# Layer 3 attention: score groups of three heads across key tiles, one exponential over three PSUM banks

## Chip, cores and metric

The kernel runs on one core of one Trainium2 chip. The metric is the device time of one execution in microseconds; it is the time from the first to the last instruction of that core, plus a few microseconds of start.

## The reference

Four layers, each added to its input `x` of shape (2, 128, 64, 64). Only the last one is touched. It normalizes `x` by groups, projects it to queries, keys and values of eight heads with 16 channels each, and attends over all S = 4096 places:

```python
def _L3_conv_ref(x, wq, bq, wk, bk, wv, bv):
    ...
    a = jnp.einsum('bhcq,bhck->bhqk', q, k) / jnp.sqrt(jnp.float32(C))
    a = jax.nn.softmax(a, axis=-1)
    o = jnp.einsum('bhqk,bhck->bhcq', a, v)
    return o.reshape(B, C, h, w)
...
x = x + _L3_conv_ref(_gn(x), L3_conv_wq, L3_conv_bq, L3_conv_wk, L3_conv_bk, L3_conv_wv, L3_conv_bv)
```

## The kernel before

Layer 3 starts at about 2290 us of the span and lasts to its end. `_layer3` goes through four attentions one after the other: batch b in 0, 1 and half t in 0, 1, a half being four of the eight heads. For each, `queries_and_keys` makes `q` (two tiles, the rounded query and its remainder) and `k`, in which head j lies in the partitions 32j to 32j + 31; `values` makes `vt`, the transposed values, each head with a block of ones beside it, so that the sum of the weights comes out of the same matmul.

`attend` then loops over 8 blocks of 512 queries (qb) and, inside, over 32 tiles of 128 keys (kt): 256 key tiles per attention, 1024 in all. A key tile has three steps.

- `scores` (matmul at L2060): for both query parts n and the four heads j, keys (32 partitions by 128 columns, stationary) times queries (32 by 512, moving). n = 0 starts a sum and n = 1 ends it. Two PSUM tiles `ps_s` of two banks each take the four heads' results. The four matmuls of one n use four different strips of 32 rows of the array.
- the exponential (L2070, ScalarE): one activation for each of the two PSUM tiles, 128 partitions by 1024 columns, to a tile `weights` in SBUF.
- `multiply` (L2079): for the four heads, values (128 partitions by 32 columns, stationary) times weights (128 by 512), added up over the 32 key tiles in one bank of `ps_acc`; head j uses columns 32j to 32j + 31 of the array.

PSUM has three score tiles of two banks (pool `f3_sp`) and two accumulators of one bank (`f3_acc`). Eight `weights` tiles of two banks' size stand in SBUF (`f3_p`).

The order of the instructions on each engine is that of the program: `_in_order` chains them. So TensorE gets, per key tile, the scores of kt and then the value matmuls of kt − 2:

```python
waiting.append((qb, kt, scores(qb, kt)))
if len(waiting) > 2:
    multiply(*waiting.pop(0))
yield kt if over else None
```

The preparation of the next attention is put between: before each even kt one step of `early` (the first attention's remaining keys and values), and at kt 4, 12 and 20 one step of `work()`, which yields the values (L2014), the queries and keys (L1988) and `bound`. At the end of a block of queries, `done` copies the accumulator out (L2101), divides by the sums (L2103 to L2105), adds the residual (L2106) and stores 4 pieces with DMAs of SyncE (L2108). At the end of an attention the value matmuls that still wait are issued, and the next one begins.

Of the kernel before, what the change touches and what calls it, by code (L numbers as in the profile page):

```python
# [10 lines left out]
F32 = mybir.dt.float32  # L11
AF = mybir.ActivationFunctionType
ALU = mybir.AluOpType
AX = mybir.AxisListType
PSUM = bass.MemoryType.PSUM
# [3 lines left out]
CH = 512  # L19
NCH = S // CH  # L20
ROWS = CH // W
NQT = S // 128
# [1894 lines left out]
    nc.vector.tensor_scalar_mul(l3["b_qk"], l3["b_qk"], scales)  # L1917


@with_exitstack  # L1920
def _layer3(ctx, tc, X, l3, cst, out, worst, here):
    nc = tc.nc
# [2 lines left out]
    ctx.enter_context(_in_order(tc))  # L1925
    one = ctx.enter_context(tc.tile_pool(name="f3_one", bufs=1))
    two = ctx.enter_context(tc.tile_pool(name="f3_two", bufs=2))
    pp = ctx.enter_context(tc.tile_pool(name="f3_p", bufs=8))
    spp = ctx.enter_context(tc.tile_pool(name="f3_sp", bufs=3, space=PSUM))
    accp = ctx.enter_context(tc.tile_pool(name="f3_acc", bufs=2, space=PSUM))  # L1930

    def acc():
        return accp.tile([128, CH], F32, tag="acc", name="ps_acc")
# [118 lines left out]
    def attend(b, t, q, k, vt, early):  # L2052
        ac = [None]

        def scores(qb, kt):
            ps = [spp.tile([128, 2, CH], F32, tag="sp", name="ps_s") for _ in range(2)]
            for n in range(2):
                for j in range(4):
                    rows = slice(32 * j, 32 * j + 32)
                    nc.tensor.matmul(  # L2060
                        ps[j // 2][:, j % 2, :],
                        k[rows, kt * 128 : (kt + 1) * 128],
                        q[n][rows, qb * CH : (qb + 1) * CH],
                        start=(n == 0),
                        stop=(n == 1),
                    )
            w = []
            for p in range(2):
                w.append(pp.tile([128, 2, CH], F32, tag="weights", name="weights"))
                nc.scalar.activation(w[p], ps[p], AF.Exp)  # L2070
            return w

        def multiply(qb, kt, w):
            if kt == 0:
                ac[0] = acc()
            for j in range(4):

                i = j % 2
                nc.tensor.matmul(  # L2079
                    ac[0][32 * j : 32 * j + 32, :],  # L2080
                    vt[:, kt, j // 2, i : i + 2, :].rearrange("p a d -> p (a d)"),
                    w[j // 2][:, i, :],
                    start=(kt == 0),
                    stop=(kt == NQT - 1),
                )
            if kt == NQT - 1:
                done(qb, ac[0])

        def done(qb, ps):
            cols = slice(qb * CH, (qb + 1) * CH)  # L2090

            places = [
                (slice(32 * j + 16 * (j % 2), 32 * j + 16 * (j % 2) + 16),
                 slice(64 * t + 16 * j, 64 * t + 16 * j + 16))
                for j in range(4)
            ]
            xs = residual[qb % 2]
            for to, rows in places:
                nc.sync.dma_start(xs[to, :], X[rows, b, cols])
            u = two.tile([128, CH], F32, tag="u", name="u", bufs=1)  # L2100
            nc.vector.tensor_copy(u, ps)  # L2101
            r = two.tile([128, CH], F32, tag="r", name="r", bufs=1)
            nc.vector.stream_shuffle(r, u, [(i + 16) % 32 for i in range(32)])  # L2103
            nc.vector.reciprocal(r, r)  # L2104
            nc.vector.tensor_mul(u, u, r)  # L2105
            nc.vector.tensor_add(u, u, xs)  # L2106
            for at, rows in places:
                nc.sync.dma_start(out[b, rows, cols], u[at, :])  # L2108

        waiting = []  # L2110
        for qb in range(NCH):
            for kt in range(NQT):
                if kt % 2 == 0:
                    over = next(early, early) is early
                waiting.append((qb, kt, scores(qb, kt)))
                if len(waiting) > 2:
                    multiply(*waiting.pop(0))
                yield kt if over else None
        for x in waiting:
            multiply(*x)  # L2120

    def in_turn(*gens):
        gens = list(gens)
# [44 lines left out]
    while found:  # L2168
        b, t, got = found.pop()
        beside = up_to_next(side)  # L2170
        for kt in attend(b, t, *got):

            if kt in (4, 12, 20):
                next(beside, None)
        for _ in beside:
            pass
# [34 lines left out]
def kernel(ctx, tc, a, out):  # L2211
# [4 lines left out]
    with tc.tile_pool(name="keep", bufs=1) as keep:  # L2216
        X, cst, eps5 = _inputs(tc, keep, a)

        worst = keep.tile([128, 1 + 2 * B], F32, name="worst")
        st = keep.tile([128, B + 2, 2], F32, name="st")  # L2220
        rows_of_weights = _layer0(tc, X, a, cst, worst, st[:, :B], dram)
        with tc.tile_pool(name="late", bufs=1) as late:
            with tc.tile_pool(name="raw", bufs=1) as raw:
                l3 = _layer3_inputs(nc, late, raw, a, a["consts2"])
                _layer1(tc, X, a, cst, st[:, :B], st[:, B])
                _layer2(
                    tc,
                    X,
                    rows_of_weights,
                    cst,  # L2230
                    a["consts1"],
                    st[:, B],
                    st[:, B + 1],
                    lambda: _layer3_weights(nc, l3),
                )
            _layer3(tc, X, l3, cst, out, worst, st[:, B + 1])
        with tc.tile_pool(name="flag_ps", bufs=1, space=PSUM) as fp:
            most = keep.tile([128, 1], F32, name="most")
            nc.vector.tensor_reduce(most, worst, AX.X, ALU.max)
            pt = fp.tile([1, 128], F32, name="ps_most")  # L2240
            nc.tensor.transpose(pt, most, cst["ident"])
            top = keep.tile([1, 1], F32, name="top")
            nc.vector.tensor_reduce(top, pt, AX.X, ALU.max)
            nc.vector.tensor_scalar(within, top, LIMIT, None, ALU.is_le)
# [61 lines left out]
```

## Time and profile before

| | |
|---|---|
| time, median of 3 runs | 4274.81 us (4273.35 to 4276.23) |
| profiled execution | 4264.27 us, span 4262.5 us |
| TensorE busy | 4050.0 us, 95% of the span |
| ScalarE busy | 3340.0 us, 78% |
| VectorE busy | 2185.9 us, 51% |
| mean granted TensorE clock | 0.981 |

PE is TensorE's matmuls, PEld its weight loads, which overlap the matmuls; ACT is ScalarE, DVE is VectorE. A line of a group gives the source line, engine and operation, output and inputs with shapes, the count, then the busy time and the mean duration of one instruction, and after the second bar the idle time of the engine just before them, with what ended it. In the timeline a row gives start, length of the merged stretch, engine, line, operation and count; the length reaches to the modelled end of the last matmul, which overlaps the start of the next, so distances between starts are the better measure. A value matmul leaves two records, a score matmul one.

### The profile page before, as it was taken

To read this page: it belongs to the slowest core of one execution; us is meant where nothing else is said; L and a number is where in the kernel's file an instruction comes from. 1 tells how busy PE (TensorE), PEld (TensorE's weight loads), DVE (VectorE), ACT (ScalarE), POOL (GpSimd) and SP (SyncE) were. 2 spreads that over 40 slices of the span, in tenths; PEclk is the share of its full clock that TensorE was granted. 3 is DMA by queue.
4 is the path that set the end of the run, shared out by engine and by line. 5 is a ranking of instruction groups with operands and counts; after the bars stand their busy time and mean duration, and the time that the engine had idled before them with its cause. 6 is when DMAs were issued, how large, how long until landed. Compare 5 with 4: busy or idle time off the path is not lost. (4 is left out here: it accounts for less than half of the span.)

```text
span 4262.5 us, 82256 instructions
## 1 busy us (share of the span) xinstructions
PE 4050.0 (95%) x35790; PEld 1547.6 (36%) x35790; DVE 2185.9 (51%) x2358; ACT 3340.0 (78%) x4051; POOL 68.3 (2%) x145
## 2 busy tenths in 40 slices
PE   6899999979999997997898999999999999999998
PEld 3522222245222223444565333333333333333332
DVE  3679999836899998995775211321132012211111
ACT  4378888734888884334655999999999999999998
POOL 1001000000000001000000000000000000000000
PEclk9999999989999999998999999999999999999999
DMA  1099960000000000002670000000000000000000
GB/s 48 2 183 187 186 98 1 1 1 2 1 1 1 1 1 12 1 1 100 273 286 4 6 4 6 6 6 4 6 6 6 4 6 6 6 4 6 6 6 4
DMA packets 158822, 158.86 MB, mean 37 GB/s; under 512 B 24809, under 2 KB 148713, under 8 KB 154354
## 3 DMA queue, kind: packets, MB, share of 16 engines
q1 hardware_dynamic: 158450, 153.50, 15.2%
q8 instruction: 282, 4.62, 0.4%
q14 instruction: 90, 0.74, 0.1%
HBM read 145.09 MB, written 73.40 MB: 51 GB/s over the span
## 5 line engine op out<-in xcount | busy, mean ns | idle before, releaser
L2070 ACT ACTIVATE weights<-ps_s 128x1024 f32<-128x1024 f32 x2048 | 1884.8, 1097 | 62.8 <-PE ps_s L2060 62.3
L1330 ACT ACTIVATE weights<-ps_s 128x1024 f32<-128x1024 f32 x1024 | 992.5, 1022 | 173.2 <-PE ps_s L1321 148.2
L2079 PE MATMUL ps_acc<-weights,vt 128*32 128x512 f32 x8192 | 1092.8, 605 | 0.0
L2060 PE MATMUL ps_s<-q,k 32*128 32x512 f32 x8192 | 924.8, 444 | 5.4 <-ACT weights L2070 5.4
L1769 DVE TENSOR_TENSOR sums<-sums,weights 128x2048 f32<-128x2048 f32 x384 | 879.0, 2289 | 42.2 <-ACT weights L1330 6.2
L2060 PEld LDWEIGHTS ps_s<-q,k 32*128 32x128 f32 x8192 | 471.1, 182 | 839.4 <-ACT weights L2070 773.6
L1321 PE MATMUL ps_s<-q,k 32*128 32x512 f32 x4096 | 644.9, 640 | 3.6 <-ACT weights L1330 2.2
L2101 DVE COPY u<-ps_acc 128x512 f32<-128x512 f32 x32 | 22.1, 691 | 1039.0 <-PE ps_acc L2079 1039.0
L1734 PE MATMUL ps_acc<-weights,vt 128*32 128x512 f32 x4096 | 548.9, 605 | 3.4 <-ACT used L1759 3.2
L1321 PEld LDWEIGHTS ps_s<-q,k 32*128 32x128 f32 x4096 | 209.4, 183 | 429.7 <-issue 212.5
L2079 PEld LDWEIGHTS ps_acc<-weights,vt 128*32 128x32 f32 x8192 | 162.9, 108 | 379.4 <-issue 367.3
L1734 PEld LDWEIGHTS ps_acc<-weights,vt 128*32 128x32 f32 x4096 | 81.0, 108 | 395.1 <-issue 377.0
L655 DVE SCALAR_TENSOR_TENSOR X<-g,w,X 128x2048 f32<-128x2048 f32 x84 | 197.3, 2350 | 2.4
L1769 DVE TENSOR_TENSOR sums<-weights 128x2048 f32<-128x2048 f32 x64 | 146.5, 2289 | 60.5 <-ACT weights L1330 60.5
L1525 PE MATMUL ps_sp<-pad,diag 32*32 32x512 f32 x4608 | 166.9, 607 | 3.8 <-DVE q L1536 2.3
L988 PE MATMUL ps_z<-w_ri,e 128*32 128x128 f32 x2048 | 137.4, 408 | 13.9 <-DVE e L930 11.8
L2021 DVE TENSOR_TENSOR vt<-ps_acc,bv 128x384 f32<-128x384 f32 x32 | 17.8, 556 | 246.0 <-PE ps_acc L2014 246.0
L1503 PE MATMUL ps_sp<-xn,w_qkv 128*128 128x512 f32 x160 | 92.9, 719 | 33.7 <-DVE k L1536 16.2
L1525 PEld LDWEIGHTS ps_sp<-pad,diag 32*32 32x32 f32 x4608 | 96.1, 104 | 62.4 <-issue 16.9
L1991 DVE LOAD_MASK_SELECT qq<-ps_acc x32 | 0.4, 14 | 222.4 <-PE ps_acc L1988 222.4
L2104 DVE RECIPROCAL r<-r 128x512 f32<-128x512 f32 x32 | 107.3, 3353 | 1.1
L930 DVE TENSOR_SCALAR e<-ps_pe 32x136 f32<-32x136 f32 (+1 forms) x352 | 104.4, 297 | 5.0
(286 smaller groups left out, 2590.5 us busy)
## 6 DMA issues: line engine op xcount, KB each, us to landing
w_ri<-w_r SPq DMA_DIRECT2D x16, 2112.0 KB, 8.1
w_ri<-w_i SPq DMA_DIRECT2D x16, 2112.0 KB, 13.5
w_r<-in_L_conv_kr_w SPq DMA_DIRECT2D x15, 528.0 KB, 12.7
w_r<-in_L_conv_kr_x SPq DMA_DIRECT2D x15, 528.0 KB, 12.5
w_r<-in_L_conv_kr_y SPq DMA_DIRECT2D x15, 528.0 KB, 12.2
w_r<-in_L_conv_kr_z SPq DMA_DIRECT2D x15, 528.0 KB, 12.5
w_i<-in_L_conv_ki_w SPq DMA_DIRECT2D x15, 528.0 KB, 13.1
w_i<-in_L_conv_ki_x SPq DMA_DIRECT2D x15, 528.0 KB, 12.3
```

The lines of the kernel that those rows point to most:

```text
L655: nc.vector.scalar_tensor_tensor(xi, g[:, i : i + H // 2, j : j + W], w8[:, s : s + 1], xi, ALU.mult, ALU.add)
L930: nc.vector.tensor_scalar_mul(out, got[of, :, s], sign)
L988: nc.tensor.matmul(out.rearrange("p (n f o) -> p n f o", n=2, f=2), e[:, s, 2 * j : 2 * j + 2, :].rearrange("p f x -> p (f x)"), w.rearran ...
L1321: nc.tensor.matmul(ps[j // 2][:, j % 2, :], k[rows, kt * 128 : (kt + 1) * 128], q[rows, qb * CH : (qb + 1) * CH], start=True, stop=True,)
L1330: nc.scalar.activation(w[:, 2 * p : 2 * p + 2, :], ps[p], AF.Exp)
L1525: nc.tensor.matmul(ps[r // 2][to, r % 2, :].rearrange("p (h w) -> p h w", w=W), diag[rows, grp, t, :], pad[rows, y0 : y0 + ROWS, t % 3 : t ...
L1734: nc.tensor.matmul(ac[n][rows, :], lhs(rows), w[:, j, :], start=first, stop=last)
L1769: nc.vector.tensor_add(parts[0].rearrange("p j c -> p (j c)"), t.rearrange("p j c -> p (j c)"), w.rearrange("p j c -> p (j c)"),)
L2060: nc.tensor.matmul(ps[j // 2][:, j % 2, :], k[rows, kt * 128 : (kt + 1) * 128], q[n][rows, qb * CH : (qb + 1) * CH], start=(n == 0), stop= ...
L2070: nc.scalar.activation(w[p], ps[p], AF.Exp)
L2079: nc.tensor.matmul(ac[0][32 * j : 32 * j + 32, :], vt[:, kt, j // 2, i : i + 2, :].rearrange("p a d -> p (a d)"), w[j // 2][:, i, :], star ...
L2104: nc.vector.reciprocal(r, r)
```

## The change

The heads of successive key tiles become one stream, (qb, kt, j) with j fastest, cut into groups of three. A group may hold heads of two key tiles. `scores` makes one group: its six matmuls (two query parts, three heads) write one PSUM tile of three banks, and one activation over 1536 columns makes its weights. There are 341 such groups and one of a single head (512 columns) in each attention. `multiply` still takes the four heads of a key tile together, when all four belong to groups older than the previous one. The score pool has two tiles of three banks in place of three of two; the weights pool has five tiles of three banks' size in place of eight of two. The steps of the preparation are tied to the group in which a key tile's head 0 lies.

```diff
-    pp = ctx.enter_context(tc.tile_pool(name="f3_p", bufs=8))
-    spp = ctx.enter_context(tc.tile_pool(name="f3_sp", bufs=3, space=PSUM))
+    pp = ctx.enter_context(tc.tile_pool(name="f3_p", bufs=5))
+    spp = ctx.enter_context(tc.tile_pool(name="f3_sp", bufs=2, space=PSUM))
...
-        def scores(qb, kt):
-            ps = [spp.tile([128, 2, CH], F32, tag="sp", name="ps_s") for _ in range(2)]
-            for n in range(2):
-                for j in range(4):
+        def scores(group):
+
+            n = len(group)
+            ps = spp.tile([128, 3, CH], F32, tag="sp", name="ps_s")
+            for half in range(2):
+                for i, (qb, kt, j) in enumerate(group):
                     rows = slice(32 * j, 32 * j + 32)
                     nc.tensor.matmul(
-                        ps[j // 2][:, j % 2, :],
+                        ps[:, i, :],
                         k[rows, kt * 128 : (kt + 1) * 128],
-                        q[n][rows, qb * CH : (qb + 1) * CH],
-                        start=(n == 0),
-                        stop=(n == 1),
+                        q[half][rows, qb * CH : (qb + 1) * CH],
+                        start=(half == 0),
+                        stop=(half == 1),
                     )
-            w = []
-            for p in range(2):
-                w.append(pp.tile([128, 2, CH], F32, tag="weights", name="weights"))
-                nc.scalar.activation(w[p], ps[p], AF.Exp)
-            return w
+            w = pp.tile([128, 3, CH], F32, tag="weights", name="weights")
+            nc.scalar.activation(w[:, :n], ps[:, :n], AF.Exp)
+            return [w[:, i, :] for i in range(n)]
...
-                    w[j // 2][:, i, :],
+                    w[j],
...
-        waiting = []
-        for qb in range(NCH):
-            for kt in range(NQT):
+        heads = [(qb, kt, j) for qb in range(NCH) for kt in range(NQT) for j in range(HEADS3)]
+        waiting, over = [], False
+
+        def number(qb, kt, j):
+            return (qb * NQT + kt) * HEADS3 + j
+
+        for at in range(0, len(heads) + 2 * GROUP3, GROUP3):
+            group = heads[at : at + GROUP3]
+            begun = [kt for _, kt, j in group if j == 0]
+            for kt in begun:
                 if kt % 2 == 0:
                     over = next(early, early) is early
-                waiting.append((qb, kt, scores(qb, kt)))
-                if len(waiting) > 2:
-                    multiply(*waiting.pop(0))
+            if group:
+                waiting += zip(group, scores(group))
+            while len(waiting) >= HEADS3 and number(*waiting[HEADS3 - 1][0]) < at - GROUP3:
+                four, waiting = waiting[:HEADS3], waiting[HEADS3:]
+                multiply(*four[0][0][:2], [w for _, w in four])
+            for kt in begun:
                 yield kt if over else None
-        for x in waiting:
-            multiply(*x)
```

More of the change, by code (lines that the diff above doesn't have):

```diff
@@ L1917, in _layer3_weights @@
     nc.vector.tensor_scalar_mul(l3["b_qk"], l3["b_qk"], scales)
+HEADS3 = 4
+GROUP3 = 3
 @with_exitstack
```

## Prediction

> **What bounds the kernel now.** I read the page's groups first, then the stretch table over layer 3, then the timeline inside it. Layer 3's attention is 2048 exponentials (L2070), 8192 score matmuls (L2060) and the value matmuls (L2079, two records to a matmul):
>
> ```profile
> L2070 ACT ACTIVATE weights<-ps_s 128x1024 f32<-128x1024 f32 x2048 | 1884.8, 1097 | 62.8 <-PE ps_s L2060 62.3
> L2079 PE MATMUL ps_acc<-weights,vt 128*32 128x512 f32 x8192 | 1092.8, 605 | 0.0
> L2060 PE MATMUL ps_s<-q,k 32*128 32x512 f32 x8192 | 924.8, 444 | 5.4 <-ACT weights L2070 5.4
> ```
>
> ScalarE idles 62.8 us in all; but PE has no idle time either. One row per pair of batch and head half (b, t) says the same (columns: length, then busy us of PE, PEld, DVE, ACT, POOL, granted clock):
>
> ```profile
> 2796.00:3285.00 489.00, 485.31 (x4178) 169.30 (x4180) 103.63 (x158) 470.66 (x512) 0.55 (x1) 1.00 0.02 6
> 3285.00:3773.00 488.00, 486.46 (x4168) 168.61 (x4162) 96.21 (x135) 469.94 (x511) 0.00 (x0) 0.99 0.02 6
> ```
>
> Both engines are over 95% busy, so busy shares cannot say which one sets the pace. The timeline can. Steady state, then an interruption at 3417.08 by one `values` block (L2014):
>
> ```profile
> 3413.59 0.73 PE L2060 MATMUL ps_s<-q,k 32*128 32x512 f32 x6
> 3414.25 1.07 PE L2079 MATMUL ps_acc<-weights,vt 128*32 128x512 f32 x8
> 3415.25 0.47 PEld L2060 LDWEIGHTS ps_s<-q,k 32*128 32x128 f32 x8 [0.84 <-ACT weights L2070]
> 3415.25 0.91 PE L2060 MATMUL ps_s<-q,k 32*128 32x512 f32 x8
> 3416.09 1.06 PE L2079 MATMUL ps_acc<-weights,vt 128*32 128x512 f32 x8
> 3417.08 1.13 PE L2014 MATMUL ps_acc<-wv,X 128*128 128x96 f32 x8
> 3418.14 0.74 PE L2060 MATMUL ps_s<-q,k 32*128 32x512 f32 x8
> 3418.81 1.07 PE L2079 MATMUL ps_acc<-weights,vt 128*32 128x512 f32 x8
> 3418.98 3.77 ACT L2070 ACTIVATE weights<-ps_s 128x1024 f32<-128x1024 f32 x4 [0.86 <-PE ps_s L2060]
> 3419.81 0.98 PE L2060 MATMUL ps_s<-q,k 32*128 32x512 f32 x8
> 3420.72 1.06 PE L2079 MATMUL ps_acc<-weights,vt 128*32 128x512 f32 x8
> 3421.71 0.91 PE L2060 MATMUL ps_s<-q,k 32*128 32x512 f32 x8
> ```
>
> Read the starts. In steady state a key tile costs 1.83 us: scores to values 0.84, values to next scores 1.00; over 14 tiles (2397.06 to 2422.73 in the same view) it is 1.8336. The scores' weight loads wait there for exponentials, two per tile, so one exponential costs 0.917 and **ScalarE sets the pace**. After the interruption every exponential is ready, and PE runs free: scores to values 0.67 (3418.14 to 3418.81), values to scores 1.00 (to 3419.81), 1.67 in all. So PE is only 0.16 us per tile behind ScalarE. A gain on ScalarE beyond 9% would meet PE; a loss on PE beyond 0.16 us per tile makes PE the bound.
>
> Between two (b, t) scores follow scores, which before does only there:
>
> ```profile
> 2796.07 0.96 PE L2060 MATMUL ps_s<-q,k 32*128 32x512 f32 x10
> 2796.90 3.77 ACT L2070 ACTIVATE weights<-ps_s 128x1024 f32<-128x1024 f32 x4 [1.87 <-PE ps_s L2060]
> 2797.97 0.73 PE L2060 MATMUL ps_s<-q,k 32*128 32x512 f32 x6 [0.95 <-ACT weights L2070]
> ```
>
> From scores to their exponential 0.83; that first exponential takes 1.02 by itself, and the scores waiting for its banks start 0.05 after its end (2796.90 + 1.02 + 0.05 = 2797.97). In a narrower window the first eight matmuls last 0.74, the first four 0.51; ten last 0.96. So a round of four heads takes 0.23 (0.74 − 0.51), and the next tile follows within 0.22 when its bank is free.
>
> **What the Trainium skill says.** "TensorEngine Tiling (Array Packing)", Key Properties: tiles in different places work independently and in parallel, and a change of tiling mode drains the engine. "TensorE: Matmul & The Clock Gate", Measured speedup vs the span model: a pack lasts as long as one matmul plus about 4 ns for each further tile. The trace agrees: two of these matmuls that start together last 0.50 (3419.81), four 0.51. So a pack of three costs what a pack of four costs. "ScalarE: Activation LUTs", What ACT_TABLE_LOAD costs: an activation takes 186 ns + 0.833 ns per element, and successive ones overlap by 93 ns. The trace gives 1.02 for 1024 elements (the page 1.04) and 0.917 back to back (0.946 by the page); a 512-element copy (L1120, 586 ns) against 1022 ns for 1024 (L1330) gives 0.85 ns per element. "PSUM — Partial Sum Buffer", Terms: eight banks. Three score buffers of two plus two accumulators fill them before, two of three plus two after.
>
> **The change part by part.**
>
> *Exponentials.* 2048 of 1024 columns become 1364 of 1536 and 4 of 512. By 0.833 ns, 512 more columns cost 0.427, so one takes 1.45 alone and 0.917 + 0.427 = 1.344 back to back (1.353 by 0.85). Three key tiles hold 12 heads, four groups: 4 × 1.344 = 5.38 where 6 × 0.917 = 5.50 stood. If ScalarE stayed the bound, 0.12–0.126 × 341.3 (1024 tiles / 3) = 41–43 us saved.
>
> *Scores.* Before, three tiles are three packs of 2 rounds × 4 heads. After, four packs of 2 rounds × 3 heads. A row strip still takes its two halves one after the other: first round 0.34, the second and the turn to the value matmuls' mode 0.33. The matmul count is equal, but a pack of three leaves a quarter of the array idle, so there is one pack more per three tiles: between 0 and 0.67 more. I take 0.67, since the trace shows packs running at the time of their longest member.
>
> *Values.* Four heads still go together in `multiply`, 1.00 each, three times per four groups. The instruction order of the changed program has scores, values, scores, values, scores, scores, values: once per cycle scores follow scores directly. Without a wait that pair would be 0.56 apart (0.34 + 0.22).
>
> *The wait that is added.* Two score buffers instead of three: a group's scores need the exponential two groups earlier to be done. From scores to the scores two groups later: 0.83 + 1.45 + 0.05 = 2.33. Between groups with values in between, 2 × 1.67 = 3.34 > 2.33, so it doesn't bind. At the direct pair it does: the second group may start 2.33 after a group that lies 1.67 before the first, so 0.66–0.67 after the first instead of 0.56. Behind it on PE are its other matmuls and the next values; ScalarE waits for those scores. Cycle on PE: 3 × 1.665 + 0.67 = 5.67. ScalarE's part adds a hair: after the pair three exponentials run back to back (3 × 1.344) before the next pair's release, which gives 0.83 + 1.45 + 4.03 + 0.05 = 6.36 from a pair's first scores to the next pair's second; with the 3 × 1.665 from there to the following pair's first, two cycles take 11.36, one 5.68. So the pace becomes about **5.675 per three tiles against 5.50: 0.175 × 341.3 = +60 us**. PE, not ScalarE, then sets it, and the saving on ScalarE turns into idle time.
>
> *Insertions.* 58 blocks (`values` L2014 and queries/keys L1988) cut in. Before, one costs 0.97: from 3415.25 to 3423.55 (the start of the scores after the last line shown) four tiles take 8.30 instead of 4 × 1.833. With PE as the bound each costs its full 1.06 (3417.08 to 3418.14): 58 × 0.09 = +5 us.
>
> *At nothing.* The weights pool goes from 8 × 2 to 5 × 3 banks' worth: a buffer comes back after five groups, and its value matmuls are issued at latest two groups ahead of that reuse. Vector work, DMAs and the evacuation of L2101 keep count and order (the order shows the same rows on DVE, POOL and SP); they lie beside an attention in which DVE is busy 20–25%. The flush at the four ends of (b, t) keeps its form; its last exponential gets shorter (one head), between −1 and +1 us each, taken as 0.
>
> Sum: +65 us; carrying the same recurrence through one whole (b, t) with its starts and ends gives +67. I take +66. Against its own span: 4262.5 → 4328.5. The three timed runs have their median 12.3 above that span, so 4274.8 + 66 = **4341 us**, 1.5% slower.
>
> **Rivals.**
>
> *ScalarE stays the bound (faster).* If a pack of three cost three quarters of a pack (0.50), PE would need 4 × 0.50 + 3 × 1.00 = 5.0 < 5.38, and 42 us would be saved: 4233. For it: the page's 444 ns mean per score matmul looks like a cost per matmul. Against: four packed in 0.51, two in 0.50. It decides from a pack of 0.60 downwards (5.38 − 3.00 = 4 × 0.595).
>
> *Between (no change).* If the packs overlap at the direct pair, and strips free since the earlier group let the pair run in 0.45, the cycle is about 5.45–5.5: within 10 us, 4275. Against: the 2.33 of the wait.
>
> *The wait binds everywhere (slower still).* If a three-bank exponential held its banks longer, for example 0.2 more, the pair's second group starts 0.2 later and ScalarE's 4 × 1.54 = 6.2 per cycle becomes the bound: about +230 us. It decides from 1.42 back to back (5.675 / 4); 0.05 more on the wait alone gives +17 on top of +66. For it: no row has a 1536-column activation. Against: 512 to 1024 adds only 0.43.
>
> **How the numbers follow.** Mine 0.82; ScalarE stays the bound 0.07; between 0.05; the wait binds everywhere 0.06. Its own range: the pair at 0.56 to 0.75 moves the cycle 5.56 to 5.75 (+25 to +90); I narrow the lower end, since the wait of 2.33 is read from rows. Range 4312 to 4370. A change under 0.2% (9 us) cannot be told from none. Faster 0.08, same 0.04, slower 0.88.
>
> **What would show it.** Right: scores to values 0.67 although only six matmuls; cycles of 5.67; score loads waiting for the exponentials mainly at the direct pair; idle time before the exponentials up from 62.8 to about 130 us (in a cycle one exponential starts fresh, 1.45 + 3 × 1.344 = 5.48 of 5.675, so 0.2 × 341 = 67 more). Wrong: ScalarE idle no more than before, scores to values near 0.50, or a lone exponential far from 1.45.

## The result, and the profile after

The changed kernel takes 4340.1 us (median of four runs, 4335.8 to 4344.6) against 4274.7: a ratio of 1.0153, 95% interval 1.0135 to 1.0171. It is slower by 65 us, where 66 were forecast.

The profiled span went from 4262.5 to 4339.6. Some 8 of these 77 us lie ahead of layer 3: its first query matmul starts at 2297.8 instead of 2289.6. The code there is the same in both, and this start varies between 2289 and 2298 over all the traces below, so I don't count it to the change. From that matmul to the end of the last values it takes 2027.6 us instead of 1958.4, 69 more.

The groups of the page that answer to those of before:

```profile
L2074 ACT ACTIVATE weights<-ps_s 128x1536 f32<-128x1536 f32 x1368 | 1879.4, 1452 | 137.4 <-PE ps_s L2066 137.4
L2083 PE MATMUL ps_acc<-weights,vt 128*32 128x512 f32 x8192 | 1092.5, 606 | 0.0
L2066 PE MATMUL ps_s<-q,k 32*128 32x512 f32 x8192 | 989.1, 443 | 8.9 <-ACT weights L2074 8.2
```

A 1536-column exponential takes 1.452 us, as worked out. ScalarE's idle time before them more than doubled, from 62.8 to 137.4 us, and all of it ends with scores: it now waits for TensorE, and never for a free weights tile, though the pool has fewer of them. The timeline in steady state, of TensorE and, for the first pair of groups, of the exponential before it and the second group's weight loads:

```profile
3499.10 1.45 ACT L2074 ACTIVATE weights<-ps_s 128x1536 f32<-128x1536 f32 x1 [0.94 <-PE ps_s L2066]
3499.92 1.42 PE L2066 MATMUL ps_s<-q,k 32*128 32x512 f32 x12
3500.61 0.30 PEld L2066 LDWEIGHTS ps_s<-q,k 32*128 32x128 f32 x6 [0.39 <-ACT weights L2074]
3501.27 1.07 PE L2083 MATMUL ps_acc<-weights,vt 128*32 128x512 f32 x8
3502.27 0.74 PE L2066 MATMUL ps_s<-q,k 32*128 32x512 f32 x6
3502.93 1.07 PE L2083 MATMUL ps_acc<-weights,vt 128*32 128x512 f32 x8
3503.93 0.73 PE L2066 MATMUL ps_s<-q,k 32*128 32x512 f32 x6
3504.59 1.07 PE L2083 MATMUL ps_acc<-weights,vt 128*32 128x512 f32 x8
3505.59 1.43 PE L2066 MATMUL ps_s<-q,k 32*128 32x512 f32 x12
...
3511.28 1.42 PE L2066 MATMUL ps_s<-q,k 32*128 32x512 f32 x12
```

A row of 12 matmuls is the direct pair of groups; a row of six is one group between two blocks of values. Six matmuls to the values still take 0.66 (3502.27 to 3502.93), as eight did. From pair to pair it is 5.67 and 5.69, so 5.68 per three key tiles, where the kernel before had 5.50. The pair itself takes 1.35 to its values. Its second group's weight loads start at 3500.61, 0.69 after the first group and 0.06 after the end of the exponential whose buffer they need (3499.10 + 1.45). Over the 319 undivided pairs of the trace the medians are 0.69 and 0.05. ScalarE in the same stretch:

```profile
3500.76 5.48 ACT L2074 ACTIVATE weights<-ps_s 128x1536 f32<-128x1536 f32 x4 [0.20 <-PE ps_s L2066]
3506.43 5.48 ACT L2074 ACTIVATE weights<-ps_s 128x1536 f32<-128x1536 f32 x4 [0.19 <-PE ps_s L2066]
```

Four exponentials in 5.48, then 0.2 us without work, in each cycle. So in each cycle TensorE waits once for ScalarE, at the pair, and ScalarE once for TensorE.

### The profile page after: what moved, and what is told of

Read it like the earlier page. It is cut to its first block, busy times and chain, and to the rows that moved or that the text cites. A ratio compares the mean times of both kernels' runs of the same rounds, so it can differ in the third digit from the quotient of the medians.

```text
span 4339.6 us, 80896 instructions
## 1 busy us (share of the span) xinstructions
PE 4123.9 (95%) x35790; PEld 1494.0 (34%) x35790; DVE 2185.8 (50%) x2358; ACT 3335.0 (77%) x3371; POOL 68.2 (2%) x145
## 5 line engine op out<-in xcount | busy, mean ns | idle before, releaser
L2074 ACT ACTIVATE weights<-ps_s 128x1536 f32<-128x1536 f32 x1368 | 1879.4, 1452 | 137.4 <-PE ps_s L2066 137.4
L1330 ACT ACTIVATE weights<-ps_s 128x1024 f32<-128x1024 f32 x1024 | 992.7, 1022 | 176.4 <-PE ps_s L1321 151.5
L2066 PE MATMUL ps_s<-q,k 32*128 32x512 f32 x8192 | 989.1, 443 | 8.9 <-ACT weights L2074 8.2
L1769 DVE TENSOR_TENSOR sums<-sums,weights 128x2048 f32<-128x2048 f32 x384 | 879.2, 2289 | 44.6 <-ACT weights L1330 8.8
L2066 PEld LDWEIGHTS ps_s<-q,k 32*128 32x128 f32 x8192 | 412.5, 183 | 977.9 <-ACT weights L2074 896.0
L1321 PE MATMUL ps_s<-q,k 32*128 32x512 f32 x4096 | 648.1, 643 | 2.7 <-ACT weights L1330 1.3
L1321 PEld LDWEIGHTS ps_s<-q,k 32*128 32x128 f32 x4096 | 210.1, 184 | 431.2 <-issue 215.4
L1769 DVE TENSOR_TENSOR sums<-weights 128x2048 f32<-128x2048 f32 x64 | 146.5, 2289 | 61.3 <-ACT weights L1330 61.3
L988 PE MATMUL ps_z<-w_ri,e 128*32 128x128 f32 x2048 | 137.4, 409 | 13.9 <-DVE e L930 11.8
L1525 PEld LDWEIGHTS ps_sp<-pad,diag 32*32 32x32 f32 x4608 | 96.0, 104 | 62.8 <-issue 17.2
```

What stands on the lines that cost most here:

```text
L988: nc.tensor.matmul(out.rearrange("p (n f o) -> p n f o", n=2, f=2), e[:, s, 2 * j : 2 * j + 2, :].rearrange("p f x -> p (f x)"), w.rearran ...
L1321: nc.tensor.matmul(ps[j // 2][:, j % 2, :], k[rows, kt * 128 : (kt + 1) * 128], q[rows, qb * CH : (qb + 1) * CH], start=True, stop=True,)
L1330: nc.scalar.activation(w[:, 2 * p : 2 * p + 2, :], ps[p], AF.Exp)
L1525: nc.tensor.matmul(ps[r // 2][to, r % 2, :].rearrange("p (h w) -> p h w", w=W), diag[rows, grp, t, :], pad[rows, y0 : y0 + ROWS, t % 3 : t ...
L1769: nc.vector.tensor_add(parts[0].rearrange("p j c -> p (j c)"), t.rearrange("p j c -> p (j c)"), w.rearrange("p j c -> p (j c)"),)
L2066: nc.tensor.matmul(ps[:, i, :], k[rows, kt * 128 : (kt + 1) * 128], q[half][rows, qb * CH : (qb + 1) * CH], start=(half == 0), stop=(half ...
```

## Experiments

The theory when they began: packs of three heads cost as much as packs of four, so TensorE becomes the bound, and the two score buffers add a small wait at the direct pair. The rivals: the wide exponential or the buffers do it alone, or each matmul costs its share. Times below stand beside the kernel before on the same chip.

### A lighter exponential (e1)

```diff
-            nc.scalar.activation(w[:, :n], ps[:, :n], AF.Exp)
-            return [w[:, i, :] for i in range(n)]
+            m = min(n, 2)
+            nc.scalar.activation(w[:, :m], ps[:, :m], AF.Exp)
+            return [w[:, min(i, 1), :] for i in range(n)]
```

> The changed kernel, with the exponential over the first two of a group's three banks only; the third head takes the second one's weights (its exponential is left out, so the output is not the reference's). Matmuls as in the changed kernel. A third of ScalarE's work is gone (about 341 x 4 x 0.43 = 580 us). Theory (TensorE is the bound; the wait of the direct pair costs 0.12 of the cycle of 5.68): the wait shrinks to 0.83 + 1.02 + 0.05 = 1.90 and stops binding, the cycle is 5.00 + 0.56 = 5.56, 41 us less: 4299, still slower than before. Rival (the wide exponential or its two buffers set the pace): exponentials of 1024 back to back give 4 x 0.917 = 3.67 per cycle, so hundreds of us less, below 4000.

Measured: 4263.7 us, ratio 0.9977 (0.9968 to 0.9985), so 8 us faster than before, and 35 us less than expected. The timeline, both engines:

```profile
3503.02 0.74 PE L2066 MATMUL ps_s<-q,k 32*128 32x512 f32 x6
3503.69 1.07 PE L2084 MATMUL ps_acc<-weights,vt 128*32 128x512 f32 x8
...
3506.34 0.76 PEld L2066 LDWEIGHTS ps_s<-q,k 32*128 32x128 f32 x12 [0.84 <-issue]
3506.34 1.19 PE L2066 MATMUL ps_s<-q,k 32*128 32x512 f32 x12
3507.19 1.94 ACT L2075 ACTIVATE weights<-ps_s 128x1024 f32<-128x1024 f32 x2 [0.64 <-PE ps_s L2066]
3507.47 1.06 PE L2084 MATMUL ps_acc<-weights,vt 128*32 128x512 f32 x8
3508.46 0.73 PE L2066 MATMUL ps_s<-q,k 32*128 32x512 f32 x6
```

A third of the columns is gone from ScalarE and it idles before nearly every exponential, yet a cycle takes 5.44 (3503.02 to 3508.46): TensorE is the bound here. But the direct pair takes only 1.13 to its values (3506.34 to 3507.47), not 0.56 + 0.67 = 1.23. With no wait the second group's weights are loaded in one stretch with the first group's (the 12 loads), and no value matmuls lie between the groups. Instruction by instruction, the rounds on the two strips that both groups use start at 3506.34, 3506.68, 3506.91 and 3507.14, so the second group adds 0.23 for each of its two rounds. The extra pack is thus worth 1.13 − 0.67 = 0.46, and the wait in the changed kernel 1.35 − 1.13 = 0.22, twice what I had thought. The theory had the right total with the wrong shares.

### Two heads' scores instead of three (e2)

```diff
-                for i, (qb, kt, j) in enumerate(group):
+                for i, (qb, kt, j) in enumerate(group[:2]):
```

This stands on top of the edit of e1.

> As the run with two of three exponentials, and the third head's score matmuls are left out too: packs of two heads, four matmuls to a group (so the third head's scores are not computed; the output is not the reference's). Theory (a pack costs what its longest strip costs, whatever the number of strips): the same time as with three heads' scores, 4299 within 10 us; scores to values stay 0.66. Rival (a score matmul costs its share, 0.67 / 8 = 0.084 each): 2 x 0.084 = 0.17 less per group, 0.67 per cycle, 229 us less than that run: about 4070.

Measured: 4268.7 us, ratio 1.0013 (0.9991 to 1.0036), with more scatter (4260 to 4324). A third of the score matmuls is gone and nothing was gained over e1 (the 4299 of the theory was e1's forecast, and missed with it). In the timeline four matmuls take to the values what six and eight took, 0.66:

```profile
3500.83 0.73 PE L2066 MATMUL ps_s<-q,k 32*128 32x512 f32 x4
3501.49 1.07 PE L2084 MATMUL ps_acc<-weights,vt 128*32 128x512 f32 x8
```

So a pack of two heads costs what packs of three and four cost; the rival's 229 us are not there.

### Values in threes (e3)

```diff
...
-            while len(waiting) >= HEADS3 and number(*waiting[HEADS3 - 1][0]) < at - GROUP3:
-                four, waiting = waiting[:HEADS3], waiting[HEADS3:]
-                multiply(*four[0][0][:2], [w for _, w in four])
+            if at >= 2 * GROUP3:
+                three, waiting = waiting[:GROUP3], waiting[GROUP3:]
+                multiply(three)
```

In the part left out, `multiply` is rewritten to go through the heads it is given, whatever their key tile.

> The changed kernel, with the value matmuls issued three heads at a time, after each group, instead of four heads three times in four groups. Same matmuls in number and shape, same exponentials. Theory (packs cost the same at three as at four): four packs of 1.00 instead of three, cycle 4 x 1.665 = 6.66 against 5.68, 0.98 x 341 = 335 us more: 4675. Rival (each matmul costs its share): the direct pair and its wait are gone and nothing is added, 4295 to 4340.

Measured: 4654.9 us, ratio 1.0901 (1.0883 to 1.0919). Against the changed kernel that is 315 us more for the same matmuls, with four packs of values per cycle instead of three and no direct pair:

```profile
3500.95 0.73 PE L2066 MATMUL ps_s<-q,k 32*128 32x512 f32 x6
3501.61 1.06 PE L2082 MATMUL ps_acc<-weights,vt 128*32 128x512 f32 x6
3502.60 0.73 PE L2066 MATMUL ps_s<-q,k 32*128 32x512 f32 x6
```

Each step takes 1.65, four make 6.60; (6.60 − 5.68) × 341 = 314. A pack of three heads' values takes 0.99 (3501.61 to 3502.60) where four take 1.00, so the same holds for packs over column strips.

### Groups of two (e4 and e8)

e4 sets the group to two heads, with the score and weights buffers of before (not shown):

```diff
-GROUP3 = 3
+GROUP3 = 2
...
```

> The changed kernel's stream with groups of two heads: exponentials over two banks, three score buffers of two banks and eight weights tiles, all as before; only the scores are issued in packs of two heads instead of four. Theory (the loss comes from packs that fill fewer strips): the second pair's strips are free, so its first round can lie beside the first pair's second: 0.34 + 0.23 + 0.33 = 0.90 and 1.90 for a key tile against 1.833, about 69 us more than before: 4345; if the two packs do not overlap, 1.13 and 2.13 a tile, +300: 4575. Rival (the wide exponential or the two buffers cause the loss): as before, 4275.

Measured: 4370.8 us, ratio 1.0233 (1.0216 to 1.0250). The size is near the theory's first figure (4345), but the trace shows another reason:

```profile
3500.37 0.74 PE L2066 MATMUL ps_s<-q,k 32*128 32x512 f32 x8
3501.05 1.23 PE L2083 MATMUL ps_acc<-weights,vt 128*32 128x512 f32 x8
3502.20 0.81 PE L2066 MATMUL ps_s<-q,k 32*128 32x512 f32 x8
```

Both packs of two together reach their values in 0.68, the time of one pack: they lie on four different strips. It is the values that take 1.15 instead of 1.00. They need the exponential of two groups earlier, which with groups of two is the newest but one, and they wait for it: the first two heads' values start at 3501.05, the other two's at 3501.22, when that exponential has just ended. My edit had shortened that distance, so e4 doesn't answer the question it was made for. e8 restores the distance (the loop's range, not shown, is two groups longer too):

```diff
...
-            while len(waiting) >= HEADS3 and number(*waiting[HEADS3 - 1][0]) < at - GROUP3:
+            while len(waiting) >= HEADS3 and number(*waiting[HEADS3 - 1][0]) < at - 3 * GROUP3:
```

> The stream in groups of two, as in the run with pairs, but a key tile's value matmuls are issued two groups later, so that their exponentials are done as long before as in the kernel before. Theory (in the run with pairs the two packs lay on four different strips and cost one pack, 0.67; its loss came from value matmuls that waited for the newest exponentials): back to the kernel before, 4275, plus up to 15 us because steps of the preparation now fall between the two packs of a key tile. Rival (packs of two cost a pack each): 4345 or more, as in the run with pairs.

Measured: 4300.5 us, ratio 1.0067 (1.0041 to 1.0092): 70 us less than e4, but 26 more than before, above the 15 I had allowed. In steady state a key tile takes what it took before. Only where a step of the preparation falls between a tile's two packs do the packs cost 0.66 each:

```profile
3499.94 0.73 PE L2066 MATMUL ps_s<-q,k 32*128 32x512 f32 x4
3500.60 1.13 PE L2018 MATMUL ps_acc<-wv,X 128*128 128x96 f32 x8
3501.66 0.73 PE L2066 MATMUL ps_s<-q,k 32*128 32x512 f32 x4
3502.33 1.07 PE L2083 MATMUL ps_acc<-weights,vt 128*32 128x512 f32 x8
...
3506.89 0.91 PE L2066 MATMUL ps_s<-q,k 32*128 32x512 f32 x8
3507.73 1.07 PE L2083 MATMUL ps_acc<-weights,vt 128*32 128x512 f32 x8
3508.72 0.91 PE L2066 MATMUL ps_s<-q,k 32*128 32x512 f32 x8
```

A tile takes 1.83 (3506.89 to 3508.72). There are 48 tiles in the trace that values or queries and keys split so, and 48 × 0.66 = 32 us; layer 3 is 1990.9 us long here, 32.5 more than before, and the medians differ by 26. That the split tiles account for all of it is an estimate from this count. So it is not the number of heads in a pack that counts, but how often the engine starts a pack anew or a strip is used again.

### Where the wait begins (e9)

```diff
-            nc.scalar.activation(w[:, :n], ps[:, :n], AF.Exp)
-            return [w[:, i, :] for i in range(n)]
+            m = min(n * CH, 1280)
+            flat = [x.rearrange("p a c -> p (a c)")[:, :m] for x in (w, ps)]
+            nc.scalar.activation(*flat, AF.Exp)
+            return [w[:, min(i, 1), :] for i in range(n)]
```

> The changed kernel with each exponential over 1280 of the 1536 columns; the third head takes the second one's weights (half of its exponentials are left out and the others unused, so the output is not the reference's). From scores to the scores two groups later: 0.83 + 1.235 + 0.05 = 2.12. Theory (what the two score buffers cost is a wait with a threshold: it binds only above 1.67 + 0.46, when the second group's loads can not be made ahead): at 1280 columns the wait is just gone, the cycle is 5.44 as with 1024 columns, 4264 within 8 us. Rival (the time follows the length of the exponential): half of the way from 4264 to 4340, 4302.

Measured: 4269.6 us, ratio 0.999 (0.998 to 0.9999), 6 us above e1 and 32 below the halfway mark. In its timeline the cycle is 5.46 (3500.32 to 3505.78) and the pair takes 1.14 to its values. From 1024 to 1280 columns next to nothing happens; from 1280 to 1536 the whole 70 us come. That is a wait with a threshold, not work that adds up.

### ScalarE's side (e7)

```diff
-            nc.scalar.activation(w[:, :n], ps[:, :n], AF.Exp)
+            nc.scalar.activation(w[:, : min(n, 2)], ps[:, : min(n, 2)], AF.Exp)
+            if n == 3:
+                nc.scalar.activation(w[:, 2], ps[:, 2], AF.Exp)
```

> The changed kernel, with each group's exponential cut into one over two banks and one over the third; packs and buffers stay. ScalarE's saving is taken back and more: 0.917 + 0.49 = 1.41 per group. Theory (TensorE is the bound, ScalarE has 0.2 idle per cycle): only the direct pair's wait grows, by 0.06 and by 3 x 0.063 in the chain of exponentials over two cycles; the cycle is 5.74 to 5.80, +20 to +41 us: 4360 to 4381. Rival (ScalarE's total is the bound): 4 x 0.063 = 0.25 per cycle, +86 us: 4426.

Measured: 4386.3 us, ratio 1.0278 (1.0261 to 1.0295), 46 us above the changed kernel: just over the theory's upper figure (41), and 40 under the rival's.

```profile
3523.84 1.51 PE L2066 MATMUL ps_s<-q,k 32*128 32x512 f32 x12
3525.28 1.07 PE L2085 MATMUL ps_acc<-weights,vt 128*32 128x512 f32 x8
```

The pair takes 1.44 to its values here, and 1.48 in the mean over the trace, against 1.35 in the changed kernel; (1.48 − 1.35) × 341 = 44. What grows is the loop from scores through exponentials to scores.

### Is the saving there when TensorE has room? (e5, e6, e10, e11)

First I made the values cheaper, in both kernels alike:

```diff
-vt = two.tile([128, NQT, 2, 3, 16], F32, tag="vt", name="vt")
+vt = two.tile([128, NQT, 2, 3, 16], mybir.dt.bfloat16, tag="vt", name="vt")
```

and the weights tiles in bf16 too (not shown).

> The kernel before, with layer 3's weights and values kept in bf16, which changes the rounding of these two operands; the value matmuls get cheaper. The reference point for the changed kernel with the same edit. Theory: ScalarE is the bound already, 0.917 per exponential, so a key tile stays at 1.833; the insertions find slack on TensorE and most of the 62.8 us of ScalarE's idle time goes: 4215 to 4240. Rival (TensorE is the bound before): the time falls by several hundred us.

> The changed kernel with layer 3's weights and values in bf16, the same rounding change. Theory (ScalarE's saving is real and hidden behind TensorE): now ScalarE sets the pace at 4 x 1.344 = 5.38 per three key tiles, 0.12 x 341 = 41 us under the kernel before with the same edit, less up to 25 us for insertions that two buffers absorb worse; 4185 to 4215. Rival (the wide exponential or two buffers cost time by themselves): no faster than the kernel before with bf16 values.

Measured: 4512.1 (1.0561, 1.0543 to 1.0579) and 4541.8 us (1.0631, 1.0613 to 1.0648). Both are slower than with fp32 values. The stretch table gives it away; the last column but two is the granted clock, here of e5:

```profile
4000.00:4100.00 100.00, 100.00 (x590) 43.96 (x586) 9.04 (x11) 94.33 (x98) 0.00 (x0) 0.50 0.02 4
```

TensorE ran layer 3 at half its clock (0.50 to 0.52 in three such stretches of each kernel), and was the bound in both. The pair says nothing about ScalarE's saving. A second pair makes room in another way, with only the first query part in the scores (shown as it stands in the changed kernel; in the one before the loop is over `n`):

```diff
-            for half in range(2):
+            for half in range(1):
...
-                        stop=(half == 1),
+                        stop=True,
```

> The kernel before, with only the first of the two query parts in the scores (the queries' remainder is left out, which changes the rounding of the scores). TensorE gets slack: scores to values about 0.44. Theory (ScalarE is the bound): a key tile stays at 1.833; only the insertions are absorbed a little better, 0.2 to 0.3 of 58: 4255 to 4265. If the granted TensorE clock falls, as it did with bf16 values, this pair says nothing. Rival (TensorE is the bound before): 0.23 x 1024 = 235 us less.

> The changed kernel with the same part left out of the scores. TensorE's cycle with its wait is 3 x 1.44 + 0.66 = 4.98 < 5.38. Theory (ScalarE's saving is real and was hidden by the extra pack and the wait): ScalarE sets the pace at 5.38 per three tiles, 41 us under the kernel before with the same edit, less up to 25 for insertions that two buffers absorb worse: 4220 to 4250. Rival (wide exponentials or two buffers bring nothing in any case): not below the kernel before with the same edit.

Measured: 4248.7 us (0.9939, 0.9917 to 0.9962) and 4210.5 us (0.985, 0.9825 to 0.9876), each a little below the range I had given. The clock stayed at 1.00 in the stretch from 4000 to 4100 us. The changed kernel is now 38 us faster than the one before with the same edit, where 41 less some insertions were expected; its ScalarE idles 43.4 us only, and its exponentials' busy time is 1844.1 against 1884.9 in the kernel before with the same edit:

```profile
L2074 ACT ACTIVATE weights<-ps_s 128x1536 f32<-128x1536 f32 x1368 | 1844.1, 1605 | 43.4 <-PE ps_s L2066 43.4
```

The saving is real. It needs room on TensorE. e11 is the fastest of all kernels here, but at another rounding of the scores, so it is not a replacement for either.

## Why the prediction was right, point by point

- **What bounds before.** ScalarE, with TensorE 0.16 us per tile behind. e10 bears it out: 4096 of the 8192 score matmuls gone, and 26 us gained where 235 would have come had TensorE been the bound, most of it in idle time of ScalarE (62.8 to 35.9).
- **Exponentials.** 1.45 alone was forecast, 1.452 measured. The 41 to 43 us of saving appear in e10 against e11 (38).
- **Pace.** 5.675 per three tiles was forecast, 5.68 measured. The sum of +66 us stands against +65 in the medians and +69 in layer 3 of the two profiles.
- **Who sets the pace.** "PE, not ScalarE, then sets it" is only half true. TensorE alone would take 5.44 to 5.46, as e1 and e9 show. In the changed kernel each engine waits for the other once per cycle, and the loop between them sets the 5.68. The sum held that loop (the 2.33 and the 6.36); the sentence behind it did not.
- **Shares within the pace: the step that failed.** I took the extra pack at a full 0.67, and the pair without a wait at 0.56 between its groups, 0.56 + 0.67 to its values, a cycle of 5.56; that left 0.11 for the wait. e1 and e9 show 1.13 and 5.44 to 5.46. The right split of the 0.68 above three packs of four (5.00) is 0.46 for the pack and 0.22 for the wait. This matters for the story: without the wait the cycle would be under the 5.50 of before, and the kernel about level with it (4264 to 4270). The extra pack brings TensorE to 5.44 to 5.46, so that little is left of ScalarE's saving (5.38 against 5.50); **the wait for one of two score buffers makes the loss**. My total was saved since the wait is measured from the group two places earlier, so it didn't contain the wrong term.
- **The rival "between"** put the pair without a wait at 0.45 and the cycle at 5.45 to 5.5. It had that price nearly right and was beaten only by the 2.33 of the wait, the argument I had set against it.
- **Insertions** at +5 were not measured by themselves; the rest of layer 3 (69 − 0.18 × 341 = 8 us) leaves room for that size.
- **ScalarE's idle time.** About 130 forecast, 137.4 measured.
- **A sign that I chose badly.** Score loads were to wait for exponentials mainly at the direct pair. The table of waits charges 896 us to them, 1216 times. Most of that is the load queue standing still while the value matmuls run: in e1 the loads behind values stand still for the same 0.84 with the exponential long done. The label names the last semaphore, not what held it up. The distance between starts was the usable sign.

Not tried: the full exponential with three buffers of three banks, since nine banks for the scores and two for the accumulators don't fit. So the price of the wait with full exponentials rests on the difference between 1.35 and 1.13 in the traces and on e9.

## What to carry to other kernels

Before regrouping work so that one engine gets larger instructions, count how often the packed engine must start a pack. In these runs heads left out of a pack saved nothing (0.66 us with 8, 6 or 4 matmuls), and the strips that two groups in a row both used cost two rounds more, one for each query part (2 × 0.23). Larger tiles at the same memory mean fewer of them in flight; measure the loop from filling a buffer to its release, and compare it with the distance between its users. Here that wait began at a threshold (none at 1280 columns) and then cost its full excess (0.21 more exponential, 0.21 more at the pair). And make room on the second engine first: the same change gained 38 us as soon as there was some.

## What the runs showed that I had not expected

- Matmuls on a free strip were not held up by earlier ones on a busy strip. In e4 the program issues both rounds of the first pack and then the second pack, yet four matmuls stand together at the start (3500.37, 0.51 long) and all eight end after 0.74. I had expected 0.90 to the values.
- Cheaper value matmuls made the kernel 239 us slower, since the granted clock fell to 0.50 in layer 3 (mean 0.752 against 0.981). TensorE was over 95% busy there, at that clock. The Trainium skill, "TensorE: Matmul & The Clock Gate", Part 1, ties the clock to TensorE's activity: half rate by default and after an idle window, full rate after a busy one. The trace shows that half rate, but not the idle window: in e5 the clock falls at 2358.6 us, and stays there but for short returns, while TensorE's records have no gap over 1.5 us from 2303 us on. What in this stream brought it about was not settled; halving the number of score matmuls (e10, e11) left the clock at 1.00.
